# Down projection of a mixture-of-experts layer: the short rests of the contraction on two halves of the array

## The chip, the cores and the metric

The kernel runs on one core of one Trainium2 chip. A core has a matrix engine (PE, with its weight loads shown apart as PEld), three engines for elementwise work (DVE, ACT, POOL), a queue that issues DMAs (SP; POOL issues the indirect ones), on-chip memory of 128 partitions (SBUF) and accumulators that the matrix engine writes (PSUM, eight banks of 512 f32 values per partition). The metric is the device time of one execution in microseconds, the median of several runs; less is better.

## The reference, cut to what matters

The program has four stages: a quantized gated linear layer, a feed-forward layer whose weights come from a lookup table, a selective state-space scan, and a mixture of experts. The change lies in the last one. There, 2048 tokens of 512 values choose 8 of 32 experts each; an expert is a gated layer with an inner width of 192:

```python
HIDDEN, INTER, N_EXPERTS, TOP_K = 512, 192, 32, 8
probs = jax.nn.softmax(x @ gate_w, axis=-1)
w, sel = jax.lax.top_k(probs, K)
...
g = jnp.einsum('ech,ehi->eci', xg, w_gate)
u = jnp.einsum('ech,ehi->eci', xg, w_up)
y = jnp.einsum('eci,eih->ech', jax.nn.silu(g) * u, w_down).reshape(E * C, H)
out = jnp.zeros((T + 1, H), x.dtype).at[t_slot].add(w_slot[:, None] * y)
```

`xg` are the rows of an expert's tokens. The third product, with `w_down`, is the down projection: a contraction over 192 = 128 + 64 inner values. All of it is in f32.

## The kernel before

The inputs come in four batches of 512 tokens. The quantized layer and the lookup layer run first, woven into each other; then the scan of each batch is woven with the feed-forward layer (tiles `pgu`, `po_f`) and with the routing of the batch before. A scheduler orders the instructions of each engine from the order in which the program records them and from the dependences of tiles; each engine then works through its own queue in order.

An expert is worked on in calls. In the early stage, from about 1214 us, eight experts are called for the tokens of the first half (320 slots each), woven with the gate and the routing of the last batch. The late stage, from about 1404 us, has 32 calls: 24 of 576 slots, and the eight early experts again with 320 slots for the tokens of the second half. The first sixteen late calls alternate between 576 and 320 slots, then sixteen of 576 follow.

A call (`expert`) has four steps, separated by `yield`:

1. Loads. The weights of gate and up go into `w` (name `egu`), those of down into `wd` (name `ed`): rows 0 to 127 in `wd[:, 0, :]` (L810), the other 64 rows in partitions 64 to 127 of `wd[:, 1, :]` (L811). POOL gathers the token rows block by block, 128 slots each, the last block 64 (`xg`, L816).
2. Each block is transposed on PE (`pt_g`, L829) and copied by ACT or DVE in turn into `xT` (`exT`, L831).
3. Gate and up (`pg`, L841). The 384 columns of weights make three groups of 128: the first 128 of gate, a middle group with the 64 rests of gate and of up, and the first 128 of up. A call of 576 slots does this in two parts of 288. ACT and DVE then make the activation `h` (`eh`, L852 to L854): 128 inner values in `h[:, 0, :]`, the 64 rests in partitions 64 to 127 of `h[:, 1, :]`.
4. Down (`po_e`, L859). For each block two products of 128 partitions with 512 columns add up in one bank. In the second one partitions 0 to 63 are zero on both sides. ACT (even blocks) or DVE (odd ones) scales the result by the token's gate into `y` (`ey`, L862, L864), and POOL adds it with an indirect DMA (`sums`, L865) to one of two arrays in device memory: even blocks to `sums0`, odd ones to `sums1`. The last call but one sends its last block to `sums1`, the last call all its blocks.

`pipeline` interleaves the calls: the loads run two calls ahead, and the transposes of call i+1 are recorded between the gate and up of call i and its down projection. At the end `add_sums` (L896 to L902) adds both arrays to the residual; the reading of `sums0` is woven with the last call, that of `sums1` comes last.

The zeros are written once: `expert_buffers` makes three buffers `ed` and two `eh` by hand and clears their lower half with five memsets on POOL (L791); `expert` takes them in turn. PSUM banks come from rings by tag: in the late stage three banks `t` (for `pt_g` and `po_e`) and five `g` (for `pg`).

Of the kernel before, what the change touches and what calls it, by code (L numbers as in the profile page):

```python
# [16 lines left out]
F32 = mybir.dt.float32  # L17
# [4 lines left out]
AF = mybir.ActivationFunctionType  # L22
ALU = mybir.AluOpType
# [4 lines left out]
P = 128  # L28
NB = 4
S = 512  # L30
HID = 512
# [16 lines left out]
SLOTS = 576  # L48
# [10 lines left out]
class Kernel:  # L59
# [723 lines left out]
        nc.vector.tensor_scalar(self.more, pc[:, :1], 0.0, None, ALU.is_gt)  # L783

    def expert_buffers(self, ep):

        nc = self.nc
        self.ed = [ep.tile([P, 2, HID], F32, name=f"ed{i}", bufs=1) for i in range(3)]
        self.eh = [ep.tile([P, 2, SLOTS], F32, name=f"eh{i}", bufs=1) for i in range(2)]
        for b in self.ed + self.eh:  # L790
            nc.gpsimd.memset(b[: P // 2, 1, :], 0.0)  # L791
        self.turn = 0
        self.gu_tag = "m"

    def expert(self, ep, e, at, col, n, sums):


        nc, t = self.nc, self.t
        R = EI - P
        xln, tokens, to, lo = at  # L800
        self.turn += 1

        w = ep.tile([P, KH, 2 * EI], F32, tag="egu", name="egu", bufs=3)
        up = t["w_up"][e].rearrange("(k p) i -> p k i", p=P)
        nc.sync.dma_start(out=w[:, :, :EI], in_=t["w_gate"][e].rearrange("(k p) i -> p k i", p=P))
        nc.sync.dma_start(out=w[:, :, EI : 2 * P], in_=up[:, :, P:])
        nc.sync.dma_start(out=w[:, :, 2 * P :], in_=up[:, :, :P])

        wd, h = self.ed[self.turn % 3], self.eh[self.turn % 2]
        nc.sync.dma_start(out=wd[:, 0, :], in_=t["w_down"][e, :P, :])  # L810
        nc.sync.dma_start(out=wd[P - R :, 1, :], in_=t["w_down"][e, P:, :])  # L811
        blocks = [(b, min(P, n - b)) for b in range(0, n, P)]
        rows = []
        for j, (b, m) in enumerate(blocks):
            xg = ep.tile([P, ROW], F32, tag="xg", name="xg", bufs=10)
            nc.gpsimd.indirect_dma_start(  # L816
                out=xg[:m, :],
                out_offset=None,
                in_=xln,
                in_offset=bass.IndirectOffsetOnAxis(ap=tokens[:m, lo + j, col : col + 1], axis=0),  # L820
            )
            rows.append(xg)
        yield
        xT = ep.tile([P, KH, SLOTS], F32, tag="exT", name="exT")
        gates = ep.tile([P, len(blocks)], F32, tag="gates", name="gates", bufs=3)
        for j, (xg, (b, m)) in enumerate(zip(rows, blocks)):
            pt = self.bank("t", "pt_g")
            for k in range(KH):
                nc.tensor.transpose(pt[:, k * m : (k + 1) * m], xg[:m, k * P : (k + 1) * P], self.ident[:m, :m])  # L829
            copy = nc.vector.tensor_copy if j % 2 else nc.scalar.copy  # L830
            copy(xT[:, :, b : b + m], pt[:, : KH * m].rearrange("p (k w) -> p k w", k=KH))  # L831
            nc.scalar.copy(gates[:m, j : j + 1], xg[:m, HID + e : HID + e + 1])
        yield
        parts = 1 + (n > HID)
        hs = n // parts
        for z in range(0, n, hs):
            pg = [None] * 3
            for i in (1, 0, 2):
                pg[i] = self.bank(self.gu_tag, f"pg{i}")
                for k in range(KH):  # L840
                    nc.tensor.matmul(  # L841
                        pg[i][:, :hs],
                        lhsT=w[:, k, i * P : (i + 1) * P],
                        rhs=xT[:, k, z : z + hs],
                        start=k == 0,
                        stop=k == KH - 1,
                    )
            for dst, gate, up in (
                (h[P - R :, 1, z : z + hs], pg[1][:R, :hs], pg[1][P - R :, :hs]),
                (h[:, 0, z : z + hs], pg[0][:, :hs], pg[2][:, :hs]),  # L850
            ):
                nc.scalar.activation(dst, gate, AF.Tanh, scale=0.5)  # L852
                nc.vector.scalar_tensor_tensor(dst, dst, 1.0, gate, ALU.add, ALU.mult)  # L853
                nc.vector.scalar_tensor_tensor(dst, dst, 0.5, up, ALU.mult, ALU.mult)  # L854
        yield
        for j, (b, m) in enumerate(blocks):
            po = self.bank("t", "po_e")
            for k in range(2):
                nc.tensor.matmul(po[:m, :], lhsT=h[:, k, b : b + m], rhs=wd[:, k, :], start=k == 0, stop=k == 1)  # L859
            y = ep.tile([P, HID], F32, tag="ey", name="ey", bufs=4)  # L860
            if j % 2:
                nc.vector.tensor_scalar(y[:m, :], po[:m, :], gates[:m, j : j + 1], None, ALU.mult)  # L862
            else:
                nc.scalar.activation(y[:m, :], po[:m, :], AF.Copy, scale=gates[:m, j : j + 1])  # L864
            nc.gpsimd.indirect_dma_start(  # L865
                out=sums[j],
                out_offset=bass.IndirectOffsetOnAxis(ap=to[:m, lo + j, col : col + 1], axis=0),
                in_=y[:m, :],
                in_offset=None,
                compute_op=ALU.add,  # L870
            )
        yield

    def pipeline(self, experts):
# [84 lines left out]
def tile_kernel(ctx: ExitStack, tc: tile.TileContext, t: dict):  # L959
    k = Kernel(tc, t)  # L960
    k.constants(ctx)
    scan = ExitStack()
    with ExitStack() as early:
        k.banks(early, t=2, m=2, y=2, d=2)
        with ExitStack() as ffn:
# [15 lines left out]
            for b in range(NB):  # L981
                n = steps + (4 if b == 0 else 0)
# [9 lines left out]
        ep = ctx.enter_context(tc.tile_pool(name="ep", bufs=2, side="right"))  # L992
        k.expert_buffers(ep)
        full, nc = SLOTS // P, tc.nc
# [1 line left out]
        first = k.pipeline(k.expert(ep, e, (k.xln[0], *at, 0), e, ROOM[0], two) for e in range(EARLY))  # L996
        weave((chain(k.gate(mp, NB - 1), k.route(rp, NB - 1)), KH + routes), (first, 2 * EARLY))
    scan.close()
    k.banks(ctx, t=3, g=5)
    k.gu_tag = "g"  # L1000
    tp = ctx.enter_context(tc.tile_pool(name="tp", bufs=6))
    rows = k.table_rows(ep, "exT", k.tables[0] + k.tables[1], SLOTS, EARLY, NE, SLOTS)
# [8 lines left out]
    sums = [two] * (len(calls) - 2) + [two[:4] + k.sums[1:], k.sums[1:] * 5]  # L1011
# [60 lines left out]
```

## Time and profile before

Three runs took 2131.37, 2130.96 and 2122.72 us; the median is 2130.96. The profile is of one execution of 2123.81 us.

| what | value |
|---|---|
| profiled execution | 2123.81 us, of it span 2121.9 us |
| PE busy | 1847.6 us, 87% of the span |
| DVE, ACT, POOL busy | 1239.2 (58%), 663.6 (31%), 971.8 us (46%) |
| L841 `pg`, PE | 1536 instructions, 397.5 us busy |
| L859 `po_e`, PE | 672 instructions, 307.5 us busy |
| L829 `pt_g` on the chain that ended last | 3% of the span |
| L865 `sums`, POOL | 168 issues, 260.7 us busy, 130.5 us idle before them until an earlier one had landed |
| `ed` loads | 40 of the upper rows, 40 of the rests |

The page of a profile gives each engine's busy time, the span in 40 slices, the DMA queues, the chain of work that ended last, and the costliest groups of instructions. A group's row names its line, engine, output and inputs, the partitions and elements of each, how many there are, and what the engine waited for before them. In the matmul rows `128*64` stands for 128 rows of the array (the contraction) by 64 columns (the output's partitions). Instructions of PE overlap, so their mean length is more than the time from one start to the next, which is what a queue of them takes; that is read from a timeline. A few records of matmuls and loads are missing from any trace.

### The profile page before, as it was taken

What the parts mean: (1) busy time and instruction counts of PE and PEld (TensorE: products, weight loads), DVE (VectorE), ACT (ScalarE), POOL (GpSimd) and SP (SyncE); (2) the same over time, 40 slices, a digit from 0 to 9 for tenths busy, and PEclk for the clock granted to TensorE, in tenths of its full rate; (3) what the DMA queues carried; (4) which work ended last, traced back from release to release, by engine and by line L of the source; (5) the groups of instructions that cost most, each with busy time, mean ns of one, the idle gap of its engine ahead of it and who ended that gap; (6) DMA issues with size and microseconds to landing.
All of it is one profiled execution on the core that took longest, in us unless ns stands there. A gap on an engine that the chain in (4) does not pass through costs nothing.

```text
span 2121.9 us, 23529 instructions
## 1 busy us (share of the span) xinstructions
PE 1847.6 (87%) x8367; PEld 1104.3 (52%) x8377; DVE 1239.2 (58%) x2029; ACT 663.6 (31%) x1251; POOL 971.8 (46%) x841
## 2 busy tenths in 40 slices
PE   4777859998988998898979979779999999999980
PEld 2443437543644655374636545456656566666650
DVE  6788743599988878987899754122222222222241
ACT  1553441433433334333523232112222222222210
POOL 3111001166338742775067756645555555555431
PEclk9899969999999998899999999869999999999995
DMA  8421106045325532452235586558787877777765
GB/s 260 113 98 54 70 8 225 32 129 129 100 62 112 109 84 60 111 107 72 82 71 117 103 226 141 102 144 179 165 171 163 168 174 150 165 158 151 143 129 178
DMA packets 184499, 266.06 MB, mean 125 GB/s; under 512 B 43138, under 2 KB 89698, under 8 KB 184372
## 3 DMA queue, kind: packets, MB, share of 16 engines
q1 hardware_dynamic: 142628, 180.12, 31.0%
q0 software_dynamic: 41744, 84.34, 21.8%
q8 instruction: 68, 1.11, 0.2%
q14 instruction: 59, 0.48, 0.1%
HBM read 203.68 MB, written 69.18 MB: 129 GB/s over the span
## 4 chain that ended last, share of the span: by engine, by line
PE 36%; DMA 9%; DVE 6%; issue 3%; POOL 3%; ACT 1%; SPq 0%; DVEq 0%; POOLq 0%; ACTq 0%
PE pg L841 16%; PE po_e L859 12%; PE pt_g L829 3%; DMA sums<-ey,to 3%; DMA bc<-xdbl 3%; DVE st L493 2%; POOL dBu L492 1%; DMA acc<-sums 1%; POOL table L707 1%; PE pgu L371 1%; DVE sc L495 1%; PE po_f L387 1%; DMA table<-i_tok,to 1%; DMA xg<-xln,tokens 1%; ACT st L490 1%
## 5 line engine op out<-in xcount | busy, mean ns | idle before, releaser
L841 PE MATMUL pg<-exT,egu 128*128 128x288 f32 (+1 forms) x1536 | 397.5, 417 | 0.1
L492 POOL TENSOR_TENSOR dBu<-dtu,bc 128x512 f32<-128x512 f32 x256 | 322.9, 1276 | 150.7 <-DMA bc<-xdbl 100.4
L865 POOL DMA_INDIRECT sums<-ey,to x168 | 260.7, 1552 | 228.4 <-DMA sums<-ey,to 130.5
L841 PEld LDWEIGHTS pg<-exT,egu 128*128 128x128 f32 x1536 | 289.0, 191 | 116.6 <-issue 30.3
L493 DVE TENSOR_TENSOR_SCAN st<-st,dBu 128x512 f32<-128x512 f32 x256 | 308.4, 1222 | 55.8 <-POOL dBu L492 28.8
L859 PE MATMUL po_e<-ed,eh 128*128 128x512 f32 (+1 forms) x672 | 307.5, 605 | 6.9 <-DVE eh L854 3.8
L496 PE MATMUL py<-sc,ident 128*128 128x512 f32 x512 | 267.4, 638 | 47.7 <-DVE sc L495 46.6
L490 ACT ACTIVATE st<-dt,A 128x512 f32<-128x512 f32 x256 | 170.7, 686 | 391.0 <-DVE sc L495 374.2
L816 POOL DMA_INDIRECT xg<-xln,tokens x168 | 163.7, 974 | 162.0 <-PE pt_g L829 107.6
L853 DVE SCALAR_TENSOR_TENSOR eh<-eh,pg 64x288 f32<-64x288 f32 (+3 forms) x128 | 58.9, 460 | 245.3 <-ACT eh L852 245.1
L859 PEld LDWEIGHTS po_e<-ed,eh 128*128 128x128 f32 (+1 forms) x672 | 113.4, 178 | 169.8 <-issue 164.0
L332 PE MATMUL pw<-oh,lut_t 128*32 128x344 bf16 (+1 forms) x2052 | 132.2, 377 | 71.2 <-DVE oh L326 70.8
L371 PE MATMUL pgu<-xT,wg 128*128 128x256 f32 (+1 forms) x704 | 182.3, 396 | 1.4 <-DVE o L238 0.5
L496 PEld LDWEIGHTS py<-sc,ident 128*128 128x128 f32 x512 | 93.8, 198 | 163.8 <-DVE sc L495 113.9
L371 PE MATMUL pgu<-xT,wu 128*128 128x256 f32 (+1 forms) x704 | 178.7, 393 | 0.0
L495 DVE TENSOR_TENSOR sc<-st,bc 128x512 f32<-128x512 f32 x256 | 167.6, 679 | 5.2 <-PE py L496 0.5
L371 PEld LDWEIGHTS pgu<-xT,wg 128*128 128x128 f32 (+1 forms) x704 | 133.9, 195 | 60.4 <-issue 39.9
L862 DVE TENSOR_SCALAR ey<-po_e,gates 128x512 f32<-128x512 f32 x64 | 48.0, 750 | 199.9 <-PE po_e L859 183.0
L387 PE MATMUL po_f<-wd,h 128*128 128x512 f32 (+1 forms) x352 | 163.2, 601 | 0.0
L864 ACT ACTIVATE ey<-po_e,gates 128x512 f32<-128x512 f32 (+1 forms) x104 | 71.3, 685 | 285.5 <-PE po_e L859 203.6
L371 PEld LDWEIGHTS pgu<-xT,wu 128*128 128x128 f32 (+1 forms) x704 | 137.6, 197 | 33.3 <-issue 12.4
L707 POOL DMA_INDIRECT table<-i_tok,to x128 | 126.8, 991 | 34.3 <-issue 24.2
(254 smaller groups left out, 1931.0 us busy)
## 6 DMA issues: line engine op xcount, KB each, us to landing
bc<-xdbl SPq DMA_DIRECT2D x128, 512.0 KB
egu<-in_w_gate SPq DMA_DIRECT2D x40, 384.0 KB
ix<-idx_b SPq DMA_DIRECT2D x16, 688.0 KB
egu<-in_w_up SPq DMA_DIRECT2D x40, 256.0 KB
ed<-in_w_down SPq DMA_DIRECT2D x40, 256.0 KB
sums<-zero SPq DMA_DIRECT2D x2, 4608.0 KB
acc<-sums SPq DMA_DIRECT2D x16, 512.0 KB
xln<-xn_r SPq DMA_DIRECT2D x24, 256.0 KB
```

The lines of the kernel that those rows point to most:

```text
L371: nc.tensor.matmul(pg[:m, j * W : (j + 1) * W], lhsT=w[:, k, c * P : c * P + m], rhs=xT[:, k, :], start=k == 0, stop=k == KH - 1,)
L387: nc.tensor.matmul(po, lhsT=h[:m, c, i * P : (i + 1) * P], rhs=self.wd[:m, c, :], start=c == 0, stop=c == NIC - 1,)
L490: nc.scalar.activation(st, dt[:, e, :], AF.Exp, scale=self.A[:, e, n : n + 1])
L492: nc.gpsimd.tensor_tensor(dBu, dtu[:, e, :], bc[:, 0, :], ALU.mult)
L493: nc.vector.tensor_tensor_scan(st, st, dBu, 0.0, ALU.mult, ALU.add)
L495: nc.vector.tensor_tensor(sc, st, bc[:, 1, :], ALU.mult)
L496: nc.tensor.matmul(py[e], lhsT=self.ident, rhs=sc, start=n == 0, stop=n == NST - 1)
L707: scatter = nc.gpsimd.indirect_dma_start(out=tables[k % len(tables)], out_offset=bass.IndirectOffsetOnAxis(ap=to[:, i, k : k + 1], axis=0) ...
L816: nc.gpsimd.indirect_dma_start(out=xg[:m, :], out_offset=None, in_=xln, in_offset=bass.IndirectOffsetOnAxis(ap=tokens[:m, lo + j, col : co ...
L841: nc.tensor.matmul(pg[i][:, :hs], lhsT=w[:, k, i * P : (i + 1) * P], rhs=xT[:, k, z : z + hs], start=k == 0, stop=k == KH - 1,)
L859: nc.tensor.matmul(po[:m, :], lhsT=h[:, k, b : b + m], rhs=wd[:, k, :], start=k == 0, stop=k == 1)
L865: nc.gpsimd.indirect_dma_start(out=sums[j], out_offset=bass.IndirectOffsetOnAxis(ap=to[:m, lo + j, col : col + 1], axis=0), in_=y[:m, :], ...
```

## The change

The buffers with zeros go: `ed` and `eh` become ordinary tiles from rings of three and two, and the five memsets are dropped. The 64 rests of the down weights are loaded twice, into partitions 0 to 63 and 64 to 127 of `wd[:, 1, :]`. The activation of a rest is written to the lower half for the first blocks of a call (`low`: two of five blocks, one of three) and to the upper half for the others. The parts of a 576-slot call become 256 and 320 slots; in a 320-slot call the rest is written in two pieces.

The down projection goes by groups: blocks 0 and 2, then 1, 3 and 4; in a call of three blocks all three. A group first does the products of 128 inner values, each into a bank of its own, then the products of 64 inner values, each on the half of the partitions where its operands lie, then the evictions and scatter-adds. The late stage has four banks `t` and four `g`.

```diff
-        self.ed = [ep.tile([P, 2, HID], F32, name=f"ed{i}", bufs=1) for i in range(3)]
-        self.eh = [ep.tile([P, 2, SLOTS], F32, name=f"eh{i}", bufs=1) for i in range(2)]
-        for b in self.ed + self.eh:
-            nc.gpsimd.memset(b[: P // 2, 1, :], 0.0)
-        self.turn = 0
...
-        wd, h = self.ed[self.turn % 3], self.eh[self.turn % 2]
+        wd = ep.tile([P, 2, HID], F32, tag="ed", name="ed", bufs=3)
+        h = ep.tile([P, 2, SLOTS], F32, tag="eh", name="eh")
         nc.sync.dma_start(out=wd[:, 0, :], in_=t["w_down"][e, :P, :])
-        nc.sync.dma_start(out=wd[P - R :, 1, :], in_=t["w_down"][e, P:, :])
+        for r in (0, P - R):
+            nc.sync.dma_start(out=wd[r : r + R, 1, :], in_=t["w_down"][e, P:, :])
...
-        parts = 1 + (n > HID)
-        hs = n // parts
-        for z in range(0, n, hs):
+        low = len(blocks) // 2 * P
+        for z, hs in ((0, low), (low, n - low)) if n > HID else ((0, n),):
...
+            cut = max(low - z, 0)
+            rest = [(r, a, b) for r, a, b in ((0, 0, min(cut, hs)), (P - R, cut, hs)) if a < b]
             for dst, gate, up in (
-                (h[P - R :, 1, z : z + hs], pg[1][:R, :hs], pg[1][P - R :, :hs]),
+                *(
+                    (h[r : r + R, 1, z + a : z + b], pg[1][:R, a:b], pg[1][P - R :, a:b])
+                    for r, a, b in rest
+                ),
                 (h[:, 0, z : z + hs], pg[0][:, :hs], pg[2][:, :hs]),
             ):
...
-        for j, (b, m) in enumerate(blocks):
-            po = self.bank("t", "po_e")
-            for k in range(2):
-                nc.tensor.matmul(po[:m, :], lhsT=h[:, k, b : b + m], rhs=wd[:, k, :], start=k == 0, stop=k == 1)
+        half = len(blocks) // 2
+        groups = [[j, half + j] for j in range(half)]
+        if len(blocks) % 2:
+            groups[-1].append(len(blocks) - 1)
+        for group in groups:
+            po = {}
+            for j in group:
+                b, m = blocks[j]
+                po[j] = self.bank("t", "po_e")
+                nc.tensor.matmul(po[j][:m, :], lhsT=h[:, 0, b : b + m], rhs=wd[:, 0, :], start=True, stop=False)
+            for j in group:
+                b, m = blocks[j]
+                r = 0 if b < low else P - R
+                nc.tensor.matmul(
+                    po[j][:m, :], lhsT=h[r : r + R, 1, b : b + m], rhs=wd[r : r + R, 1, :], start=False, stop=True
+                )
+            for j in group:
...
-    k.banks(ctx, t=3, g=5)
+    k.banks(ctx, t=4, g=4)
```

More of the change, by code (lines that the diff above doesn't have):

```diff
@@ L785, in expert_buffers @@
     def expert_buffers(self, ep):
-        nc = self.nc
-        self.ed = [ep.tile([P, 2, HID], F32, name=f"ed{i}", bufs=1) for i in range(3)]
-        self.eh = [ep.tile([P, 2, SLOTS], F32, name=f"eh{i}", bufs=1) for i in range(2)]
-        for b in self.ed + self.eh:
-            nc.gpsimd.memset(b[: P // 2, 1, :], 0.0)
-        self.turn = 0
         self.gu_tag = "m"
@@ L800, in expert @@
         xln, tokens, to, lo = at
-        self.turn += 1
         w = ep.tile([P, KH, 2 * EI], F32, tag="egu", name="egu", bufs=3)
@@ L855, in expert @@
         yield
-        for j, (b, m) in enumerate(blocks):
-            po = self.bank("t", "po_e")
-            for k in range(2):
[L859 to L871, printed above, removed]
+        half = len(blocks) // 2
[15 more added lines that the diff above has]
+            for j in group:
+                b, m = blocks[j]
+                y = ep.tile([P, HID], F32, tag="ey", name="ey", bufs=4)
+                if j % 2:
+                    nc.vector.tensor_scalar(y[:m, :], po[j][:m, :], gates[:m, j : j + 1], None, ALU.mult)
+                else:
+                    nc.scalar.activation(y[:m, :], po[j][:m, :], AF.Copy, scale=gates[:m, j : j + 1])
+                nc.gpsimd.indirect_dma_start(
+                    out=sums[j],
+                    out_offset=bass.IndirectOffsetOnAxis(ap=to[:m, lo + j, col : col + 1], axis=0),
+                    in_=y[:m, :],
+                    in_offset=None,
+                    compute_op=ALU.add,
+                )
         yield
```

## The prediction

> **What bounds the kernel now.** I read the busy times of the page, then busy time by stretch, then the chain of waits inside the longest stretch. The expert products run from 1.24 ms to the end; in 1405 to 2036 us PE never stops:
>
> ```profile
> core 0: us, PE busy (x) PEld busy (x) DVE busy (x) ACT busy (x) POOL busy (x), PEclk, DMA share, GB/s
> ...
> 1405.00:2036.00 631.00, 631.00 (x2405) 396.79 (x2404) 176.67 (x328) 162.54 (x419) 341.49 (x274) 0.99 0.76 160
> 2036.00:2090.00 54.00, 30.23 (x92) 15.92 (x90) 16.31 (x21) 6.15 (x12) 15.35 (x10) 0.86 0.57 123
> ```
>
> PE is busy 631 of 631 us; DVE (28%) and ACT (26%) have room. The chain there is PE alone (pg, pt_g, po_e in turn). So 22 calls of five blocks and 8 of three are worth what PE's queue takes. In the last 54 us PE is idle almost half the time, and POOL's chain of scatter-adds decides.
>
> The timeline of PE shows one call of three blocks and one of five (start, duration, instructions merged):
>
> ```profile
> 1550.51 5.56 PE L859 MATMUL po_e<-ed,eh 128*128 128x512 f32 x12
> 1556.00 11.91 PE L841 MATMUL pg<-exT,egu 128*128 128x288 f32 x48
> 1567.74 1.43 PE L829 MATMUL pt_g<-ident,xg 128*128 128x128 f32 x12
> 1569.10 8.99 PE L859 MATMUL po_e<-ed,eh 128*128 128x512 f32 x20
> 1578.02 6.73 PE L841 MATMUL pg<-exT,egu 128*128 128x320 f32 x24
> ```
>
> Start to start, the down projection takes 5.49 us for three blocks and 8.92 us for five. Two products per block would be 6 and 10; the trace has 12 and 20 instructions, so each f32 product is two passes with a weight load each. The loads show what a pass and a change of array shape cost:
>
> ```profile
> 1611.11 0.19 PEld L859 LDWEIGHTS po_e<-ed,eh 128*128 128x128 f32 x1 [0.24 <-issue]
> 1611.54 0.19 PEld L859 LDWEIGHTS po_e<-ed,eh 128*128 128x128 f32 x1 [0.24 <-issue]
> 1612.49 0.19 PEld L859 LDWEIGHTS po_e<-ed,eh 128*64 128x64 f32 x2 [0.76 <-issue]
> 1612.97 0.14 PEld L859 LDWEIGHTS po_e<-ed,eh 128*64 128x64 f32 x1 [0.29 <-issue]
> ```
>
> A pass is 0.429 us (1611.11 to 1611.54). The next load shown is two passes on (one record is missing) and 0.09 late, and its first pass is 0.05 longer (1612.49 to 1612.97): going to 64 columns costs 0.14. Rows behave likewise, seen where the scan's 16-row product comes between full ones:
>
> ```profile
> 395.03 0.29 PEld L466 LDWEIGHTS pd<-xd,dt_w 16*128 16x128 f32 x2 [0.33 <-ACT xd L456]
> 395.56 0.18 PEld L466 LDWEIGHTS pd<-xd,dt_w 16*128 16x128 f32 x1 [0.24 <-issue]
> 395.99 0.18 PEld L466 LDWEIGHTS pd<-xd,dt_w 16*128 16x128 f32 x1 [0.24 <-issue]
> 396.94 0.73 PEld L371 LDWEIGHTS pgu<-xT,wu 128*128 128x128 f32 x4 [0.76 <-issue]
> ```
>
> Its first pass takes 0.53, 0.10 over (a load of 128 columns that nothing hides), and the way back is again 0.09 late (395.99 to 396.94, two passes), and the first po_e pass after a change takes 697 ns where others take 592, the same 0.10. So a change costs 0.20 into a shape of 128 columns, 0.14 into 64. Check: 20 x 0.429 + 0.34 = 8.92, and 12 x 0.429 + 0.34 = 5.49, as measured.
>
> **The passes.** In the built program five blocks go: upper products of 0 and 2; rests of 0 and 2; upper of 1, 3, 4; rests of 1, 3, 4. Three: upper of 0, 1, 2; rests 0, 1, 2. A rest still streams 512 columns in two passes, so only overlap can save. In the queue stand a1 a2 b1 b2. If matmuls start in order, a2 waits for a1 (same rows), b1 starts beside a2, b2 follows: three passes for four. Each pair saves one, 0.43: two pairs in five blocks, one in three.
>
> That side by side works at all, the lookup stage shows, on column tiles:
>
> ```profile
> 122.15 1.35 PE L332 MATMUL pw<-oh,lut_t 128*32 128x344 bf16 x32
> ```
>
> 32 matmuls in 1.35 us is 0.04 each; in the same timeline a bf16 matmul of 512 columns on the full array (po at L234) follows its like after 0.21, which would make 0.14 for 344 columns; so four run at once. Here single-pass matmuls alternate between tiles; no row shows two-pass ones on row tiles. The Trainium skill ("TensorE: Matmul & The Clock Gate", section "Measured speedup vs the span model") has a pack take one matmul's time plus about 4 ns for each further tile: two passes saved for every pair. The same page ("The mechanism") says matmuls start and end strictly in program order, which speaks against this change: a2 stands between a1 and b1. By the first rule pairs save 104 passes over the 52 pairs of the window, 44.6 us; by the second 22.3. I take the second. Bounds: 0 and 44.6.
>
> **The changes of shape.** Before, each call has one change to 64 columns and one back: 0.34. After, five blocks have six: to row tiles 0.20, back 0.20, to 64 columns 0.14, from there to row tiles 0.20, the 64-column rest of block 4 0.14, back 0.20: 1.08. Three blocks have four: 0.14 + 0.20 + 0.14 + 0.20 = 0.68. The two steps between narrow shapes are in no row; bounds 0 and 0.20 each, and I take the nearest rows. The skill's "TensorEngine Tiling (Array Packing)", section "Key Properties", says only that changing the mode drains the array, with no price; a drain alone would be the 0.09, and the row adds the bare load.
>
> **Sum for the window.** Five blocks: 18 x 0.429 + 1.08 = 8.80 (saves 0.12). Three: 11 x 0.429 + 0.68 = 5.40 (saves 0.09). 22 x 0.12 + 8 x 0.09 = **3.4 us**. Most of the gain goes into changes of shape.
>
> **What lies beside it.** Parts of 256 and 320 columns stream as many as two of 288: nothing. Three more elementwise instructions in a call of three blocks lie under pg (6.6 us of PE). Four pg banks for five: the fourth bank starts part two and pg1's bank is free long before pg0 asks; cover about 1.7 us, else that much per call. The upper product of block 2 needs the second part of eh earlier; its last DVE step (0.46) ends under pt_g (1.36). The second copy of the rest adds 128 KB and about 0.5 us of SP per call, at a DMA share of 0.76: hidden; loads run calls ahead. Evictions come in groups; a fourth t bank holds them. POOL's scatters go to sums 0, 0, 1, 0, 1 instead of 0, 1, 0, 1, 0; three on sums 0, about 5.6 us each, fit the 23 us of a call.
>
> **The start.** The memsets go from POOL, where they stood ahead of the first gather:
>
> ```profile
> 1213.89 1.44 POOL L791 MEMSET ed<- 64x512 f32 x3 [0.38 <-PE po_f L387]
> 1215.28 1.09 POOL L791 MEMSET eh<- 64x576 f32 x2
> 1216.54 1.01 POOL L816 DMA_INDIRECT xg<-xln,tokens  x1 [0.17 <-issue]
> ```
>
> That is 2.5 us, on the chain (the scan's ACT waits behind a gather). But three more gathers (1.27 each) now stand ahead of the scan's next dBu on POOL. Bounds -2.5 and +1.3; I take -1. The early eight calls save nothing: until 1390 POOL with its table scatters is what the chain follows.
>
> **The tail.** POOL's timeline from the last call but one:
>
> ```profile
> 2039.18 1.57 POOL L865 DMA_INDIRECT sums<-ey,to  x1 [10.40 <-ACT ey L864]
> 2041.05 1.56 POOL L865 DMA_INDIRECT sums<-ey,to  x1 [0.30 <-DVE ey L862]
> 2044.77 1.56 POOL L865 DMA_INDIRECT sums<-ey,to  x1 [2.16 <-DMA sums<-ey,to]
> 2046.98 1.56 POOL L865 DMA_INDIRECT sums<-ey,to  x1 [0.65 <-issue]
> 2052.84 1.42 POOL L865 DMA_INDIRECT sums<-ey,to  x1 [4.30 <-DMA sums<-ey,to]
> 2062.13 1.56 POOL L865 DMA_INDIRECT sums<-ey,to  x1 [7.87 <-ACT ey L864]
> ```
>
> Scatters on one array wait for each other. Before: 0, 1, 0, 1, 1, then five on sums 1, landed at 2089.5. After: 0, 0, 1, 1, 1. The first comes 1.06 later (an upper product and a change stand ahead); the second is 5.6 behind it; so the first on sums 1 goes at 2047.8 instead of 2041.05. Two more intervals, 5.9 and (beside the loads of sums 0) 8.6, and one of 5.9, put the last call's first scatter at 2068.1, 6 us late; 1.3 come back because its second y is no longer waited for. Loss **4.7**, bounds 1.6 (no contention) and 7.
>
> Total: 2121.9 - 3.4 - 1 + 4.7 = 2122.2 of span, 2124 with the 1.9 outside it. The profiled execution (2123.8) is 7 below the median of the runs, 2131; no change there means **2130**.
>
> **Rivals.** (A) In order, as above: shape bounds move it by -9 to +3, start and tail by -5 to +5; own range 2118 to 2143. Chance 0.66. (B) The two halves are wholly independent, b1 beside a1: 22.3 us more, five blocks in 7.94, three in 4.97: 2108. For it: the column tiles and the span rule. Against: the two passes. 0.19. (C) No overlap for two-pass f32: nothing saved and the changes paid, 9.66 and 5.83: 22.3 worse, 2153, **slower**. It decides once a pair's four passes take over 1.35 us (1.72 less the 0.37 of added changes per pair). For it: no row-tile overlap is in this trace. 0.15.
>
> A measurement here can tell about 0.5% (11 us) from no change. A puts 0.07 below, 0.53 within, 0.06 above; with B and C: faster 0.26, same 0.53, slower 0.21. The range takes in A and nearly all of B.
>
> **What would show it.** Down-projection stretches of 8.80 and 5.40 (A), 7.94 and 4.97 (B), 9.66 and 5.83 (C); starts of the rests' passes at 0, 0.53, 0.53, 0.96 under A; PE idle in 1405 to 2036 would mean a bank or scatter bound I priced at nothing; the last call's first scatter some 6 us later behind its po_e.

## The result and the profile after

The changed kernel takes 2109.36 us (median of six runs, 2101.0 to 2113.53), the kernel before beside it 2126.39 us (six runs, 2120.07 to 2131.37). The ratio is 0.9914, with a 95% interval of 0.9891 to 0.9936: some 0.9% faster. The time lies inside the predicted range, but it is not the time of the likeliest case. The profiled execution takes 2106.76 us, of it 2105.0 us span, 16.9 less than before.

The first view is busy time by stretch, with the columns of the prediction's table (us, then PE, PEld, DVE, ACT and POOL busy with their instructions, clock, DMA share, GB/s). The long stretch now ends at 2018, where the last call but one starts its down projection:

```profile
1405.00:2018.00 613.00, 609.39 (x2411) 369.82 (x2409) 177.15 (x340) 159.31 (x428) 341.57 (x273) 0.99 0.78 170
2018.00:2105.00 87.00, 31.32 (x82) 14.49 (x80) 25.41 (x28) 5.63 (x10) 16.49 (x10) 0.69 0.61 173
```

PE still fills its stretch at a clock of 0.99, so the time came out of PE's own work; but 3.6 us of the 613 are idle, where before there were none (some 1.5 of them ahead of the first late `po_e`). The next view is the timeline of PE in the changed kernel (start, duration, merged instructions), over one call of three blocks and one of five; L865 are the products of 128 rows, L869 those of 64:

```profile
1547.50 2.99 PE L865 MATMUL po_e<-ed,eh 128*128 128x512 f32 x6
1550.42 2.13 PE L869 MATMUL po_e<-ed,eh 64*128 64x512 f32 x6
1552.48 11.91 PE L836 MATMUL pg<-exT,egu 128*128 128x256 f32 x48
1564.22 1.43 PE L824 MATMUL pt_g<-ident,xg 128*128 128x128 f32 x12
1565.58 1.98 PE L865 MATMUL po_e<-ed,eh 128*128 128x512 f32 x4
1567.49 1.13 PE L869 MATMUL po_e<-ed,eh 64*128 64x512 f32 x4
1568.55 2.99 PE L865 MATMUL po_e<-ed,eh 128*128 128x512 f32 x6
1571.47 2.13 PE L869 MATMUL po_e<-ed,eh 64*128 64x512 f32 x6
1573.53 1.88 PE L836 MATMUL pg<-exT,egu 128*128 128x320 f32 x6
```

The answer to the main question is in the sixth line: four passes of the rests of two blocks take 1.06 us from their start to the next product's start (1567.49 to 1568.55). Four passes one after the other with the 0.20 of a change of shape would be 1.92; two passes with it are 1.06. Start to start, five blocks take 7.95 us (1565.58 to 1573.53) and three take 4.98 (1547.50 to 1552.48). That is the prediction's case B (7.94 and 4.97), not A (8.80 and 5.40). The weight loads of another such pair show it more directly:

```profile
1532.68 0.30 PEld L869 LDWEIGHTS po_e<-ed,eh 64*128 64x128 f32 x4 [0.76 <-issue]
1533.74 0.30 PEld L865 LDWEIGHTS po_e<-ed,eh 128*128 128x128 f32 x2 [0.76 <-issue]
```

All four loads of the pair lie within 0.30 us, and the next product's come 1.06 us later. In the trace's single records the first passes of blocks 0 and 2 start at 1532.680 and 1532.686, the second ones at 1533.213 and 1533.220: each partner 6 to 7 ns behind. Counted from the first, and in the program's order a1 a2 b1 b2, that is 0, 0.533, 0.006 and 0.540 us, where case A asked for 0, 0.53, 0.53 and 0.96 us.

Where the 16.9 us of span went, cut at the first late `po_e` and at that of the last call but one (us of the profiled executions):

| part | before | after | difference | predicted |
|---|---|---|---|---|
| up to the first late `po_e` | 1423.8 | 1426.0 | +2.2 | -1 |
| from there to the last call but one | 612.4 | 589.1 | -23.3 | -3.4 (A), -25.7 (B) |
| rest, to the end of the span | 85.7 | 89.8 | +4.1 | +4.7 |

The window saves what case B has, less 2.1 us of PE idle that is new, and the tail takes 4 back.

### The profile page after: what moved, and what is told of

The parts are those of the page before. It is cut to its first block, busy times and chain, and to the rows that moved or that the text cites. A ratio compares the mean times of both kernels' runs of the same rounds, so it can differ in the third digit from the quotient of the medians.

```text
span 2105.0 us, 23555 instructions
## 1 busy us (share of the span) xinstructions
PE 1825.7 (87%) x8367; PEld 1072.7 (51%) x8377; DVE 1240.6 (59%) x2061; ACT 661.5 (31%) x1267; POOL 970.8 (46%) x836
## 5 line engine op out<-in xcount | busy, mean ns | idle before, releaser
L836 PE MATMUL pg<-exT,egu 128*128 128x320 f32 (+1 forms) x1536 | 404.4, 421 | 8.6 <-DVE eh L853 3.7
L853 DVE SCALAR_TENSOR_TENSOR eh<-eh,pg 128x320 f32<-128x320 f32 (+5 forms) x144 | 61.1, 424 | 215.1 <-ACT eh L852 120.4
L865 PE MATMUL po_e<-ed,eh 128*128 128x512 f32 (+1 forms) x336 | 171.9, 631 | 11.3 <-ACT ey L878 3.9
L496 PEld LDWEIGHTS py<-sc,ident 128*128 128x128 f32 x512 | 93.5, 197 | 162.0 <-DVE sc L495 106.6
L332 PEld LDWEIGHTS <-lut_t 128*32 128x32 bf16 x2052 | 59.8, 106 | 124.2 <-issue 84.4
```

What stands on the lines that cost most here:

```text
L332: nc.tensor.matmul(pt[i][32 * c : 32 * c + 32, :step], lhsT=self.lut_t[:, j, g, :], rhs=oh[:, c * n + i * step : c * n + (i + 1) * step], ...
L496: nc.tensor.matmul(py[e], lhsT=self.ident, rhs=sc, start=n == 0, stop=n == NST - 1)
L836: nc.tensor.matmul(pg[i][:, :hs], lhsT=w[:, k, i * P : (i + 1) * P], rhs=xT[:, k, z : z + hs], start=k == 0, stop=k == KH - 1,)
L865: nc.tensor.matmul(po[j][:m, :], lhsT=h[:, 0, b : b + m], rhs=wd[:, 0, :], start=True, stop=False)
```

## The experiments

Stretches are read from PE's timeline, start to start, as above; "window" and "tail" are the second and third row of the table. For kernels that ran several times the ratio to the kernel before is given; the others ran once. The kernel before took a median of 2124.1 to 2130.6 us beside these kernels, so their times compare by the ratio and not as they stand.

### How far the two halves are independent

That a pair overlaps leaves open why. The program holds one instruction for each f32 product, and the profile two passes. If the passes started in the program's order, b1 would have waited for a2, and it does not; but if only neighbouring products could overlap, that too would fit the changed kernel, whose pairs alternate. The first run therefore puts the two lower rests ahead of the two upper ones:

```diff
-        half = len(blocks) // 2
-        groups = [[j, half + j] for j in range(half)]
-        if len(blocks) % 2:
-            groups[-1].append(len(blocks) - 1)
+        groups = [list(range(len(blocks)))[:4], [4]] if len(blocks) > 4 else [list(range(len(blocks)))]
```

> In a call of five blocks four upper products come first, then the rests of blocks 0, 1 (lower half), 2, 3 (upper half) in this order, then block 4. Theory Q (each half of the array has its own queue, a matmul waits only for its own half, however far ahead the others stand): four passes for the four rests, a po_e stretch of 16 x 0.429 + 0.68 = 7.54 us, and the first pass of block 2 starts within 0.01 us of that of block 0. Theory N (only neighbouring products pair): 0 alone, 1 beside 2, 3 alone, six passes, 8.40 us. Theory O (passes start strictly in program order): seven passes, 8.83 us. A call of three blocks stays at 4.98 under all.

The second run has the same group in the order 0, 2, 1, 3, where lower and upper alternate:

```diff
+        groups = [[0, 2, 1, 3], [4]] if len(blocks) > 4 else [list(range(len(blocks)))]
```

> As the run with the order 0, 1, 2, 3, but the rests stand as 0, 2, 1, 3, alternating between the halves. Theories Q and N: four passes, a po_e stretch of 7.54 us for five blocks, 0.40 less than the changed kernel's 7.94 because two changes of shape fewer. Theory O: 0a, 0b beside 2a, 2b beside 1a, 1b beside 3a, 3b: five passes, 7.97 us. Over the 22 calls before the last but one, 0.40 each is 9 us off the span if nothing else waits.

The timeline of PE in the kernel with the order low, low, up, up (its L862 and L866 are the products of 128 and of 64 rows):

```profile
1644.01 3.70 PE L862 MATMUL po_e<-ed,eh 128*128 128x512 f32 x8
1647.64 1.99 PE L866 MATMUL po_e<-ed,eh 64*128 64x512 f32 x8
1649.57 1.07 PE L862 MATMUL po_e<-ed,eh 128*64 128x512 f32 x2
1650.57 1.07 PE L866 MATMUL po_e<-ed,eh 64*64 64x512 f32 x2
1651.57 6.73 PE L836 MATMUL pg<-exT,egu 128*128 128x320 f32 x24
```

and its weight loads at the rests:

```profile
1647.64 0.31 PEld L866 LDWEIGHTS po_e<-ed,eh 64*128 64x128 f32 x4 [0.76 <-DMA egu<-in_w_up]
1648.18 0.20 PEld L866 LDWEIGHTS po_e<-ed,eh 64*128 64x128 f32 x2 [0.23 <-issue]
1648.61 0.20 PEld L866 LDWEIGHTS po_e<-ed,eh 64*128 64x128 f32 x2 [0.23 <-issue]
```

Eight passes of four rests take 1.93 us (1647.64 to 1649.57), as four would (4 x 0.429 + 0.20 = 1.92), and the loads still come two at a time. The whole stretch is 7.56 us (1644.01 to 1651.57); in the alternating order it is 7.55. Overlap of neighbours alone would have given 8.40, passes in strict order 8.83. In the single records the first upper rest starts at 1647.657, 13 ns after the first lower one and 0.95 us before the second lower product, which stands ahead of it in the program (1648.606). So products start out of program order when they lie on different halves. The delay fits a hand-out in order, some 6.5 ns for each product, to a queue for each half: 13 to 14 ns behind two products, 6 to 7 behind one in the alternating order. That there are such queues is inferred from these starts; how deep they would be was not tried.

The windows are 581.8 and 580.8 us, 7 to 8 below the changed kernel's 589.1: a call of five blocks has four changes of shape instead of six. The times, 2114.82 and 2098.11 us, differ by much more than that. Up to the late stage the two have the same code, yet their first late `pg` comes at 1414.8 and at 1407.8, and the first late `po_e` 9.7 us apart; another 6.1 us lie in the tails (96.0 and 89.9), where the order of the rests may play a part. What a single run gains ahead of the late stage says nothing about the change; the windows do.

### Without overlap: all rests on one half

```diff
-            cut = max(low - z, 0)
+            cut = 0
...
-                r = 0 if b < low else P - R
+                r = P - R
```

> The changed kernel, but all rests and their activations lie on the upper half, so that no two can run side by side; the changes of shape stay. If the gain is the overlap, each pair loses two passes again: 20 x 0.429 + 1.08 = 9.66 us for five blocks and 12 x 0.429 + 0.68 = 5.83 for three; 52 pairs x 0.858 = 44.6 us more than the changed kernel, about 1.2% slower than before. If instead the gain comes from dropping the zeros or from the new order of the products, the stretches stay near 7.94 and 4.98.

```profile
1660.64 1.98 PE L865 MATMUL po_e<-ed,eh 128*128 128x512 f32 x4
1662.55 1.98 PE L869 MATMUL po_e<-ed,eh 64*128 64x512 f32 x4
1664.46 2.99 PE L865 MATMUL po_e<-ed,eh 128*128 128x512 f32 x6
1667.38 2.98 PE L869 MATMUL po_e<-ed,eh 64*128 64x512 f32 x6
1670.29 1.07 PE L836 MATMUL pg<-exT,egu 128*128 128x320 f32 x3
```

In this timeline of PE the four passes of a pair's rests take 1.91 us (1662.55 to 1664.46) in place of 1.06, although each multiplies 64 rows only. Five blocks take 9.65 us and three 5.83 (1641.71 to 1647.54), the prediction's case C. The median is 2153.09 us, ratio 1.0105 (1.0083 to 1.0127); the window is 632.8 us, 43.7 more than the changed kernel's. So dropping the zeros saves nothing by itself and costs two changes of shape per group; all of the gain is overlap.

### What a change of shape costs

The prediction took its prices from three rows. To measure them alone, the kernel before got a last block of full width, so that its down projection keeps one shape (the columns behind the call's slots hold zeros or old values, and their results are not read):

```diff
-        self.eh = [ep.tile([P, 2, SLOTS], F32, name=f"eh{i}", bufs=1) for i in range(2)]
-        for b in self.ed + self.eh:
+        self.eh = [ep.tile([P, 2, SLOTS + P // 2], F32, name=f"eh{i}", bufs=1) for i in range(2)]
+        for b in self.ed:
             nc.gpsimd.memset(b[: P // 2, 1, :], 0.0)
+        for b in self.eh:
+            nc.gpsimd.memset(b, 0.0)
...
-                nc.tensor.matmul(po[:m, :], lhsT=h[:, k, b : b + m], rhs=wd[:, k, :], start=k == 0, stop=k == 1)
+                nc.tensor.matmul(po, lhsT=h[:, k, b : b + P], rhs=wd[:, k, :], start=k == 0, stop=k == 1)
```

> The kernel before, but the last block of a call takes 128 columns of the activation instead of 64 (the other 64 rows of the bank are not read), so the array never changes shape inside the down projection. If a change to 64 columns and back costs 0.34 us as worked out, the stretches go from 8.92 to 8.58 and from 5.49 to 5.15: 30 x 0.34 = 10 us less, about 0.5% faster than before. If the late starts are no price of the shape but of something else at that place, they stay at 8.92 and 5.49.

```profile
1642.22 1.43 PE L831 MATMUL pt_g<-ident,xg 128*128 128x128 f32 x12
1643.57 8.85 PE L861 MATMUL po_e<-ed,eh 128*128 128x512 f32 x20
1652.26 6.62 PE L843 MATMUL pg<-exT,egu 128*128 128x320 f32 x24
...
1660.98 5.42 PE L861 MATMUL po_e<-ed,eh 128*128 128x512 f32 x12
1666.23 11.80 PE L843 MATMUL pg<-exT,egu 128*128 128x288 f32 x48
```

In PE's timeline of this kernel five blocks take 8.69 us and three 5.25, each 0.23 to 0.24 less than before and 0.10 to 0.11 more than the 8.58 and 5.15 expected, and the `pg` behind them takes 6.62 and 11.80 us instead of 6.73 and 11.91: the other 0.10 of the way back falls into the next line. What keeps the stretch 0.10 above its 20 passes is its first pass, which still takes 0.53 us (1643.574 to 1644.107 in the single records), behind transposes that end with 64 rows, which is a change of shape too. Transpose to transpose, this pair of calls takes 35.65 us (1642.22 to the next at 1677.87) against 36.33 before, twice 0.34. The window is 602.2 us, 10.2 below the kernel before and as expected, and the ratio is 0.995 (0.9931 to 0.9969): computing 64 output columns that nobody reads is cheaper here than changing the shape twice.

### The tail

In the changed kernel the scatter-adds of the last call but one stand so in POOL's timeline:

```profile
2019.22 1.57 POOL L879 DMA_INDIRECT sums<-ey,to  x1 [7.47 <-ACT ey L878]
2024.79 1.56 POOL L879 DMA_INDIRECT sums<-ey,to  x1 [3.99 <-DMA sums<-ey,to]
2026.66 1.56 POOL L879 DMA_INDIRECT sums<-ey,to  x1 [0.30 <-DVE eh L854]
2032.23 1.55 POOL L879 DMA_INDIRECT sums<-ey,to  x1 [4.01 <-DMA sums<-ey,to]
2041.35 1.73 POOL L879 DMA_INDIRECT sums<-ey,to  x1 [7.57 <-DMA sums<-ey,to]
2046.88 2.43 POOL L879 DMA_INDIRECT sums<-ey,to  x1 [3.81 <-DMA sums<-ey,to]
```

The first two go to one array, so the second comes 5.57 us behind the first, and the next three, on the other array, begin after it. To see whether it is this order that costs the 4 us, only the last two calls got the old order back, and with it the old work block by block:

```diff
+        if late:
+            groups = [[j] for j in range(len(blocks))]
...
-        k.expert(ep, e, (k.xln[1], *at, 0), col, n, s) for (e, at, col, n), s in zip(calls, sums)
+        k.expert(ep, e, (k.xln[1], *at, 0), col, n, s, s is not two) for (e, at, col, n), s in zip(calls, sums)
```

> The changed kernel, with the last two calls block by block as before (each block's rest follows its upper product; nothing pairs there), so that the scatter-adds of the last call but one go to sums 0, 1, 0, 1, 1 again. If the tail grew because they went 0, 0, 1, 1, 1, the stretch from the start of that call's po_e to the end of the span falls from 89.9 us to about 85.7, as before, 4 us less, though PE loses all overlap and gains changes of shape in these two calls. If the tail grew for another reason (contention, DVE's adds, the late half), it stays near 90.

POOL's timeline of this kernel, from the last call but one:

```profile
2012.85 1.57 POOL L881 DMA_INDIRECT sums<-ey,to  x1 [6.21 <-ACT ey L880]
2014.97 1.56 POOL L881 DMA_INDIRECT sums<-ey,to  x1 [0.56 <-DVE ey L878]
2018.38 1.56 POOL L881 DMA_INDIRECT sums<-ey,to  x1 [1.85 <-DMA sums<-ey,to]
2020.56 1.55 POOL L881 DMA_INDIRECT sums<-ey,to  x1 [0.61 <-issue]
2026.18 1.42 POOL L881 DMA_INDIRECT sums<-ey,to  x1 [4.07 <-DMA sums<-ey,to]
2036.39 2.19 POOL L881 DMA_INDIRECT sums<-ey,to  x1 [8.79 <-ACT ey L880]
```

The fifth scatter-add comes 13.3 us after the first instead of 22.1, and the last call's first one waits for its own result (`ey`) again, no longer for an earlier scatter-add. The tail is 86.1 us against 89.8 (85.7 expected); the window, 590.2, is unchanged. The ratio is 0.9887 (0.9866 to 0.9907), which overlaps the changed kernel's interval, so the total alone would not show 4 us. The tails of the kernels of this study agree: 89.8, 91.1 and 93.5 us with the changed kernel's groups, 84.9 to 89.3 in the seven whose last two calls go block by block. That the tail shrinks is shown; its size comes from single profiles, and kernels with the same last two calls differ by as much. Nor is the order alone: with the blocks one by one the first scatter-add also comes 0.85 us sooner after the first product (3.23 for 4.08), and the run does not part the two.

Larger groups have tails of 89.9 to 96.0, and there it is another wait: their scatter-adds alternate between the arrays, but the last call's products wait for the activation of its second part. In the kernel with the order low, low, up, up the last call's first `po_e` starts at 2040.35; from the timelines of PE and of POOL:

```profile
2047.29 3.78 PE L862 MATMUL po_e<-ed,eh 128*128 128x512 f32 x4 [4.09 <-DVE eh L854]
2053.38 1.56 POOL L876 DMA_INDIRECT sums<-ey,to  x1 [15.66 <-ACT ey L875]
```

### One group for all blocks, and what it runs into

If changes of shape are dear and any order of rests overlaps, one group with one change each way should be best. The next kernel does all products of 128 rows, then all rests, with full-width last blocks, and gives `po_e` five banks and `pg` three; the last two calls go block by block:

```diff
+        groups = [[j] for j in range(len(blocks))] if late else [list(range(len(blocks)))]
...
+                nc.tensor.matmul(po[j], lhsT=h[:, 0, b : b + P], rhs=wd[:, 0, :], start=True, stop=False)
...
+                    po[j], lhsT=h[r : r + R, 1, b : b + P], rhs=wd[r : r + R, 1, :], start=False, stop=True
...
-    k.banks(ctx, t=4, g=4)
+    k.banks(ctx, t=5, g=3)
```

> All upper products of a call, then all its rests in the order of the blocks (lower half: the first two of five or the first of three), the last block with 128 columns of the activation, five banks t and three g, and the last two calls block by block. If each half has its own queue and a change of shape costs what the loads show: 16 x 0.429 + 0.38 = 7.25 us for five blocks and 10 x 0.429 + 0.38 = 4.67 for three, 0.69 and 0.31 less than the changed kernel; over 22 and 8 calls 17.7 us, and 4 from the tail: about 2085 us, 2% faster than before. If three g banks or the bunched evictions hold PE up, the stretches are right but PE shows idle time before pg.

A second kernel is the same without the order of the last two calls:

> As the run with one group and full width, but the last two calls go in one group as well. Same stretches in the window. If the order of the scatter-adds and the time of the first y set the tail, it is longer than with the last calls block by block: the first y waits for five upper products and a rest (3.2 us later than in the kernel before), with the scatters in order 0, 1, 0, 1, 1: about 89.

The stretches came out as worked: 7.27 us (1670.18 to 1677.45) and 4.66. The kernel did not: 2176.62 us, ratio 1.0231 (1.021 to 1.0253), slower than before. Its window is 655.3 us, with 64.6 of PE idle in it; the second kernel has 659.1 and 64.9, so the tail's order is not the reason (the tails are 89.3 and 94.4, 3 to 5 us longer than expected). Two pieces of PE's timeline and then the waits of the first of the two (total us, times, longest):

```profile
1670.18 4.56 PE L868 MATMUL po_e<-ed,eh 128*128 128x512 f32 x10
1674.67 2.85 PE L872 MATMUL po_e<-ed,eh 64*128 64x512 f32 x10
1677.45 6.73 PE L842 MATMUL pg<-exT,egu 128*128 128x320 f32 x24
...
1700.56 5.14 PE L842 MATMUL pg<-exT,egu 128*128 128x320 f32 x9 [3.80 <-DVE eh L860]
```

```profile
ACT ey L881 <- DMA sums<-ey,to: 84.0, 22, 6.0
...
PE pg L842 <- DVE eh L860: 52.4, 18, 4.5
...
ACT gates L833 <- DMA xg<-xln,tokens: 43.7, 25, 5.2
```

PE waits for a bank of `pg` that the activation (`eh`) has not yet read out. The reading of these waits is that the activation is late since ACT works in order, and ahead of it stand evictions that wait for a free `ey` (five results now end at once, and four buffers are let go at the pace of the scatter-adds) and copies (`gates`) that wait for gathered rows. To tell these two apart, eight `ey` buffers instead of four:

```diff
-                y = ep.tile([P, HID], F32, tag="ey", name="ey", bufs=4)
+                y = (self.yp or ep).tile([P, HID], F32, tag="ey", name="ey", bufs=8 if self.yp else 4)
...
+    k.yp = ctx.enter_context(tc.tile_pool(name="yp", bufs=8))
```

> The run with one group, full width and five banks t, but with eight buffers ey in the late stage instead of four. In that run PE waited 52 us for DVE's eh before pg, and ACT stood before that for two reasons: a free ey (a scatter-add to land, 84 us) and the gathered rows that the gates are copied from (44 us). If the ey ring is what holds ACT, PE's waits before pg nearly vanish and the time comes to about 2085 us. If it is the gathers, which stand behind waiting scatter-adds in POOL's queue, PE's waits stay at 40 us or more and the time above 2160.

The wait of `ey` for scatter-adds is gone from ACT, `gates` still waits 49.6 us in all, and PE's idle time in the window falls from 64.6 to 30.2 us (window 618.4, one run of 2141.82 us). About half was the buffers, so neither of the two outcomes expected came about. The rest has the wait for gathered rows ahead of it, behind three banks for `pg`; which of these two bounds it was not separated.

### The banks

The same wait is in the changed kernel, in small. Its waits of PE in 1405 to 2030 us:

```profile
PE pg L836 <- DVE eh L854: 2.1, 2, 1.4
```

The next kernel is the changed one with the old ring sizes, `k.banks(ctx, t=3, g=5)`:

> The changed kernel with three banks t and five g, as before. If the 2 us that PE waits for DVE before pg in the late stage come from the fourth g bank, they go; if groups of three need the fourth t bank, PE now waits before po_e or pt_g instead, at least about 0.5 us in each call of five blocks. If the banks matter for neither, stretches stay at 7.94 and 4.98 and the window is as in the changed kernel.

PE's idle time in the window is 0.0, the window 587.0 us (589.1), and the stretches stay at 7.95 and 4.97. So those 2.1 us were the missing fifth bank of `pg`, and three banks `t` are enough for groups of two and three blocks. The one run took 2096.4 us, but its first late `po_e` comes 12 us earlier than in the changed kernel, where the scatter between runs is.

### What adds up

Two kernels put parts together. The first has the alternating group of four, full-width last blocks in calls of three, the last two calls block by block, and eight `ey` buffers:

> Rests in the order 0, 2, 1, 3 behind four upper products, then block 4 by itself with 64 columns; calls of three blocks in one group with full width; the last two calls block by block; four banks t, four g, eight ey in the late stage. From the runs so far: 7.55 us for five blocks and 4.67 for three, and a tail of about 86: 22 x 0.39 + 8 x 0.31 + 4 = 15 us less than the changed kernel, about 2092 us, a ratio near 0.984 to the kernel before. If the bunched evictions delay POOL's gathers as in the run with one group, PE waits before pg and the time stays at that of the changed kernel or above.

2099.33 us, ratio 0.9869 (0.985 to 0.9888). The tail is near the sum (87.5 us), the window is not: 582.4 us, where the sum gives 578. The wide blocks bring no gain over the alternating group alone (580.8): the stretch of three blocks falls to 4.69 us, but PE spends more on `pg`, of it 4.0 us idle in the window instead of 2.5; why was not separated, since the eight buffers and the last two calls differ too. The profiled run reached its first late `po_e` only at 1434.2, which is not explained. The second takes only the order and the tail:

```diff
+        groups = [[0, 2, 1, 3], [4]] if len(blocks) > 4 else [list(range(len(blocks)))]
+        if late:
+            groups = [[j] for j in range(len(blocks))]
```

> The changed kernel with two edits that were measured apart, and none of those that failed: groups 0, 2, 1, 3 and then 4 in calls of five blocks (the second run), and the last two calls block by block (as tried on the changed kernel). If the two add up: five blocks in 7.55 us, three in 4.98, the window from the first late po_e to the second-last call's at 581 us (changed kernel 589.1), the tail at 86 (89.8), so 12 us less than the changed kernel for the same early stage, some 2097 us, ratio to the kernel before 0.986. If the gain of one is eaten by the other (the evictions of four blocks now come together and delay the next calls, as in the kernel with one group): window above 585, PE idle before pg above 4 us, ratio 0.99 or more. The early stage is the same program as in the run with blocks 0 to 3 in one group (0, 2, 1, 3); its first late po_e was at 1425.6 there, and differs by up to 7 us between runs of one program.

2099.29 us (2092.98 to 2108.97) against 2130.54 for the kernel before, ratio 0.9842 (0.9819 to 0.9865): the lowest ratio of those measured, its interval below the changed kernel's (0.9891 to 0.9936). Window 580.0 and tail 87.0 us are as added up. Its profile is of the slowest of the five runs, 14 us later than the changed kernel at its first late `po_e`; already the last gate product of the feed-forward layer (`pgu<-xT,wg`) starts at 1196.4 us instead of 1187.5, in code that no edit touches.

## Why the prediction was right or wrong

- **The range held, the likeliest case did not.** The measured time lies below case A's own range and in the predicted one only because that was drawn to take in B.
- **The passes: wrong, and with it the likeliest case.** The step that failed is "If matmuls start in order, a2 waits for a1 (same rows), b1 starts beside a2, b2 follows: three passes for four". The runs show two for four: b1 starts 6 to 7 ns behind a1 and does not wait for a2, and the first run shows the same past a whole product. The order was applied to the passes, while the program holds whole products. The term of the sum was 22.3 us saved by overlap; its upper bound, 44.6, is what the kernel without overlap loses (43.7 in the window). Of the two rules weighed, "Measured speedup vs the span model" of the Trainium skill ("TensorE: Matmul & The Clock Gate") held, with 6 to 7 ns per product where it states about 4; "The mechanism" (matmuls start strictly in program order) did not hold across two halves. The row of the trace before, four column tiles at once, fitted both, as its tiles alternate. It could not decide between them, and 0.66 against 0.19 was more than the evidence carried.
- **The changes of shape: right.** 0.20 into 128 columns and 0.14 into 64, the unseen steps between narrow shapes among them, give 1.08 and 0.68 per call; with two passes per pair that makes 7.94 and 4.97, and 7.95 and 4.98 were measured, 9.65 and 5.83 without overlap. The 0.34 per call before was measured alone. Its check on the stretches (20 x 0.429 + 0.34) came out partly by luck: 0.10 of the way back falls into the `pg` behind, and an equal 0.10 comes in from the first pass of `po_e`, behind the 64-row transposes.
- **The sum for the window** would be 22 x 0.98 + 8 x 0.52 = 25.7 with the right number of passes; 23.3 were saved, and 2.1 of the gap is the next point. With the banks as before the window is 587.0 us, 25.4 saved, so the down projection makes up the whole gain, and that the parts of 256 and 320 columns cost nothing was right.
- **"Four pg banks for five: nothing": wrong by 2.1 us.** The wait that was to be covered comes in two of the 30 calls of the window, 0.7 and 1.4 us long. Whether the cover is 1.7 us in the other calls was not measured.
- **The start: not shown.** The first gather goes 2.0 us earlier (1214.5 for 1216.5), as dropping the memsets gives, but the late stage starts no earlier (first late `pg` 1409.5, before 1408.6). Two kernels with the same code up to there differ by 7 us, so a step of 1 us in this place can't be read from one profile.
- **The tail: right in place and near in size.** 4.1 us lost for 4.7. The last call's first scatter-add comes 5.8 us later behind the start of the last call but one, for the 6 forecast; in the trace it waits for earlier ones on its array, and block by block, with the arrays in turn, 3.7 us come back.
- **The rivals.** B was the mechanism. Its 2108 us lies at the measured 2109.36 partly by luck: it was set from 2130 for no change, while the kernel before took 2126.39 in all its runs, and the idle PE and a start without gain made up the difference. C is what comes when the halves are not both used: 2153 us forecast, 2153.09 measured beside a kernel before of 2130.61. A's own range is not the sum of the bounds named for it (2130 with -14 and +8 is 2116 to 2138, not 2118 to 2143); nothing hangs on that.

## What to carry to other kernels

Short contractions pay when two of them run on different halves of the array; a half-filled product alone took as long as a full one here, and a change of shape each way on top, so collect the pairs into few groups, but watch what the larger groups do to the work behind. In the kernel before, filling the short last block up was cheaper than changing the shape for it; together with groups of four it brought nothing. Each order of the rests that was tried overlapped, so the order may be chosen for what comes behind: evictions that came bunched waited for output buffers, and an engine that works in order passed that wait on to the work that frees the matrix engine's banks. When a stated rule and a row of the trace leave two cases open, give them chances that are not far apart.

## What the runs showed of the hardware

- Matrix products on two row halves start out of program order, 6 to 7 ns apart per product handed out, also past a product that starts only 0.95 us later. With f32 in two passes two halves gave the full factor of two: eight passes in 1.93 us, where four one after the other with a change of shape would take 1.92.
- A product with 64 output columns is a change of array shape too, and a round trip cost 0.34 us in the kernel where only the width of the last block was changed.
- The stages ahead of the late calls took 7 us longer in one of two kernels with the same code up to there (1407.8 and 1414.8), and differ by more between others; windows cut behind them repeat to within about a microsecond (580.8 and 580.0 for the same groups, 589.1 and 590.2 for those of the changed kernel). What sets this scatter was not tried.
